# Seven products instead of eight for nine more projections of a four-layer network on one core, with hand-turned PSUM rings

## The chip, the cores and the metric

The kernel runs on one core of a Trainium2 chip. A core has five engines that run their own instruction queues side by side: TensorE (PE, matrix products into PSUM), VectorE (DVE), ScalarE (ACT), GpSimd (POOL) and SyncE (SP, which only starts transfers). All arithmetic is float32. The metric is the device time of one execution in microseconds (us); the lower the better.

## The reference

The input x has 4 images of 512 channels and 32 x 32 pixels, so an image is a matrix of 512 channels by 1024 tokens. Four layers follow one another, each of the form x = x + layer(groupnorm(x)):

```python
# layer 0: attention, heads mixed before the softmax, instance norm behind it
q, k, v = w_q @ xf, w_k @ xf, w_v @ xf            # 512x512 @ 512x1024 per image
attn = einsum('bhdq,bhdT->bhqT', q, k) * scale     # 8 heads of 64 channels
attn = softmax(einsum('gh,bhqT->bgqT', w_head, attn))
attn = instance_norm(attn) * gamma + beta
out = (attn @ v).reshape(b, t, c) @ w_proj.T + b_proj
# layer 1: a gate per channel from channel means (a small simulated circuit)
# layer 2: plain attention
q, k, v = Wq @ x + bq, Wk @ x + bk, Wv @ x + bv
out = Wp @ (softmax(q.T @ k * 64 ** -0.5) @ v) + bp
# layer 3: each token reads the 8 best of 2048 memory rows
att = q @ mempool.T; vals, idx = top_k(att, 8); out = softmax(vals) @ mempool[idx]
```

## The kernel before

An image lies in on-chip memory (SBUF) as 128 partitions x 4 channel blocks x 1024 tokens. A projection of an image by a 512 x 512 weight is 32 matmul statements of 512 columns (`project`, L184; `project_tokens`, L198, for v). For float32 each statement leaves two records in the profile.

**Layer 0** runs image after image in 32 steps of 32 queries plus 7 steps of tail (`step`). A step makes scores (`scores`), copies them out on ACT, sends them to another layout through 8 transfers (into the two relay buffers of tag `s2`), mixes the heads (`mix`), takes the exponential on ACT, turns it on DVE, and multiplies it into v five steps later (`apply`). Small products of gating, sums and norms go to one PSUM bank, `pt` (`small_ps`). In the tail steps 32 to 35 the next image's q is projected (`take_q`), one quarter a step; behind the tail comes its k (`take_k`, four projections, each copied out by one DVE instruction in the order that the scores want), and on DVE the statistics of the image after that (`statistics`: rows loaded into `xs` and `o1` by ACT's queue, one at a time). v follows in the first eight steps of the next image. After image 3's tail the projections are already those of layer 2's image 0 (`take_q2`, `take_k2`, `take_v2`), and then comes layer 0's output projection for image 3 (`put_out`, 64 statements of 256 columns), whose sums go straight into rows `xr`.

**Layer 2** runs over 16 units of 4 key blocks an image (`scores2`, `apply2`): scores on PE, exponential on ACT, sums over keys on POOL and DVE. Between the images the next one's projections are made: q with eight products (`take_q2`), k, v and the output projection with seven (`seven_k`, `seven_v`, `seven_out`).

**Seven products.** A matrix product of 2 x 2 blocks normally takes 8 block products; `seven` makes it of 7, from sums and differences of the blocks of both factors (Strassen's scheme). `input_sums` makes the sums of the image's blocks and `weight_sums` those of the weight, all on DVE; `seven` then runs products 1, 4, 3, 5, 2, 7, 6, each into one PSUM pair, and adds or subtracts it into the blocks of the result: the first into a block is written by `begin` (ACT or DVE, with the bias), the others by DVE (L993). Sums of weights are stored to memory for the later images.

**PSUM** has 8 banks. In layer 0 six of them are three named pairs that the code turns by step number (`pairs[at % 3]`), one is `pv` (the product with v) and one `pt`. In layers 2 and 3 a pool of three pairs and a pool of two banks take their place, and the pool hands them out in order.

The order on each engine is the order of the program for instructions wrapped in `pin`; the others may be moved by the scheduler. A wait is a semaphore wait at the head of an instruction, and everything behind it on that engine waits too. Transfers signal on eight lanes in turn; a transfer waits until the last user of its lane has landed.

Of the kernel before, what the change touches and what calls it, by code (L numbers as in the profile page):

```python
# [16 lines left out]
P = 128  # L17
# [24 lines left out]
def fast_net(ctx: ExitStack, tc: tile.TileContext, a: dict, out: bass.AP, flag: bass.AP):  # L42
# [19 lines left out]


    def chan(src, name):
        t = const.tile([P, KC], F32, tag=name, name=name)
        nc.scalar.dma_start(out=t, in_=src)
        return t

    gamma = const.tile([P, NH], F32, tag="gamma", name="gamma")
    nc.scalar.dma_start(out=gamma, in_=a["in_gamma"].partition_broadcast(P))  # L70
    beta = const.tile([P, NH], F32, tag="beta", name="beta")
    nc.scalar.dma_start(out=beta, in_=a["in_beta"].partition_broadcast(P))
    bproj = chan(a["b_proj"], "bproj")
    bq2 = chan(a["bq"], "bq2")
    bk2 = chan(a["bk"], "bk2")
    bp2 = chan(a["bp"], "bp2")
    fcb = chan(a["fc_b"], "fcb")

    fcw = const.tile([NQ, C], F32, tag="fcw", name="fcw")
    nc.scalar.dma_start(out=fcw, in_=a["fc_w"])  # L80
    qpar = const.tile([P, NL * NQ], F32, tag="qpar", name="qpar")
    nc.scalar.dma_start(out=qpar, in_=a["q_params"].partition_broadcast(P))
# [3 lines left out]
    ident = const.tile([P, P], F32, tag="ident", name="ident")  # L86
    make_identity(nc, ident)
    ones = const.tile([P, P], F32, tag="ones", name="ones")
    nc.gpsimd.memset(ones, 1.0)
# [13 lines left out]
    )  # L103
    NS = 32
# [71 lines left out]
    def place(at, name):  # L176

        return pairs[at % 3] if at is not None else ps_s.tile([P, 2, NB], F32, tag="sc", name=name)
# [107 lines left out]

    def run_out(gen):
        for _ in gen:
            pass
# [4 lines left out]
    def first():  # L294
# [3 lines left out]
        w = I["w_q"] = eight_k([P, KC, C], "w_q0_0", 0)  # L298
        for k in range(KC):
            nc.sync.dma_start(out=xn[:, k, :], in_=x_v[0, :, k, :])  # L300
            nc.sync.dma_start(out=w[:, k, :], in_=a["w_q"][:, k, :])
        I["w_k"] = load_w("w_k", "w_k0_0", 1)
# [5 lines left out]
        def stats(k):  # L308
            mv = small.tile([P, 2], F32, tag="mv0", name=f"mv0_{k}")
            st = small.tile([P, 2, 6], F32, tag="bnst", name=f"st_a0_{k}")  # L310
            for i in range(2):
                pin(nc.vector.bn_stats(st[:, i, :], xn[:, k, i * NB:(i + 1) * NB]))
            pin(nc.vector.bn_aggr(mv, st.rearrange("p i s -> p (i s)")))
            parts[k] = group_coeffs_parts(mv[:, 0:1], mv[:, 1:2], f"a0_{k}")

        def means(k):
            next(parts[k])
            next(parts[k])

        def deviations(k):  # L320
            next(parts[k])
            found[k] = next(parts[k])
# [15 lines left out]
        stats(0)  # L338
        means(0)
        stats(1)  # L340
        deviations(0)
        means(1)
        normalize(0)
        for k in range(KC):
            if k + 2 < KC:
                stats(k + 2)
# [634 lines left out]
    def load2(b):  # L981
        for key in ("Wq", "Wk", "Wv"):
            load_sums(b, key, b == 1 or key == "Wq")

    def load_sums(b, key, plain):
        w = img[b][key] = eight_k([P, KC, C], f"{key}2_{b}")
        nc.sync.dma_start(out=w, in_=a[key] if plain else w_sums[key])

    H = C // 2
    w_sums = {key: dram.tile([P, KC, C], F32, tag=f"ws_{key}", name=f"ws_{key}")  # L990
              for key in ("Wk", "Wv", "Wp")}
# [15 lines left out]
    def weight_sums(b, key):  # L1007
# [4 lines left out]
        add7(s1, a11, a22)  # L1012
        sub7(s7, a12, a22)
        add7(a12, a11, a12)
        sub7(s6, a21, a11)
        add7(a21, a21, a22)
        nc.sync.dma_start(out=w_sums[key], in_=w)

# [14 lines left out]
    def seven(b, key, src, multiply, view, block, begin, done=None):  # L1033
# [1399 lines left out]
```

## Time and profile before

| | us |
|---|---|
| runs (3) | 2554.56, 2555.19, 2558.83; median 2555.19 |
| the profiled execution | 2558.39 |
| its span, first to last instruction | 2556.6 |

The profile is of one execution; "busy" is the time in which an engine had an instruction under way, and the granted clock of TensorE is 0.998 of full. The table gives busy us in some stretches of the span:

| stretch, us from the start | what runs | PE | DVE | ACT | POOL |
|---|---|---|---|---|---|
| 265 to 345 (80) | layer 0, from image 0 to 1 | 78.41 | 28.35 | 14.63 | 20.40 |
| 345 to 550 (205) | layer 0, image 1 | 201.40 | 161.59 | 130.13 | 110.30 |
| 1215 to 1300 (85) | from layer 0 to layer 2 | 82.68 | 35.10 | 22.61 | 23.11 |
| 1300 to 1380 (80) | layer 2, image 0 | 80.00 | 55.88 | 43.35 | 55.78 |
| 1380 to 1490 (110) | layer 2, from image 0 to 1 | 108.04 | 67.61 | 16.67 | 20.66 |
| 1600 to 1710 (110) | layer 2, from image 1 to 2 | 110.00 | 61.48 | 18.01 | 13.75 |

A line such as "PE pv L532 <- ACT pv L592: 8.9, 15, 1.6" in the list of waits says that the matmuls of line 532 waited 8.9 us in total, 15 times and at most 1.6 us, for ACT's instruction of line 592.

### The profile page before, as it was taken

To read this page: it belongs to the slowest core of one execution; us is meant where nothing else is said; L and a number is where in the kernel's file an instruction comes from. 1 tells how busy PE (TensorE), PEld (TensorE's weight loads), DVE (VectorE), ACT (ScalarE), POOL (GpSimd) and SP (SyncE) were. 2 spreads that over 40 slices of the span, in tenths; PEclk is the share of its full clock that TensorE was granted. 3 is DMA by queue.
4 is the path that set the end of the run, shared out by engine and by line. 5 is a ranking of instruction groups with operands and counts; after the bars stand their busy time and mean duration, and the time that the engine had idled before them with its cause. 6 is when DMAs were issued, how large, how long until landed. Compare 5 with 4: busy or idle time off the path is not lost.

```text
span 2556.6 us, 47828 instructions
## 1 busy us (share of the span) xinstructions
PE 2503.3 (98%) x18534; PEld 1180.8 (46%) x18534; DVE 1685.8 (66%) x2785; ACT 985.8 (39%) x1177; POOL 1192.5 (47%) x1700
## 2 busy tenths in 40 slices
PE   8999999999999999999999999999999999999998
PEld 3344534554355534555633533453353344444445
DVE  4599448872688438881267567576657648788875
ACT  1467336651666336651153145125314612121211
POOL 3266415553465425553074147117405617566655
PEclk9999999999999999999999999999999999999999
DMA  2578438872698428982301130121014046767665
GB/s 83 145 207 237 125 120 226 244 211 74 172 243 235 131 82 211 244 248 101 124 16 55 70 112 18 54 83 59 21 54 148 18 130 190 219 186 217 187 184 170
DMA packets 187211, 361.39 MB, mean 141 GB/s; under 512 B 32729, under 2 KB 96217, under 8 KB 182882
## 3 DMA queue, kind: packets, MB, share of 16 engines
q1 hardware_dynamic: 105744, 178.71, 22.6%
q0 software_dynamic: 49152, 142.79, 20.6%
q10 hardware_dynamic: 32082, 36.76, 5.3%
q8 instruction: 149, 2.44, 0.4%
q14 instruction: 84, 0.69, 0.1%
HBM read 186.96 MB, written 36.96 MB: 88 GB/s over the span
## 4 chain that ended last, share of the span: by engine, by line
PE 74%; issue 10%; POOL 7%; DVE 3%; ACT 3%; DMA 2%; POOLq 0%; SPq 0%; ACTq 0%; DVEq 0%
PE pair L192 10%; PE sc_c L1183 9%; PE pv_c L1220 9%; PE pv L532 8%; POOL got L1360 7%; PE pair L467 6%; PE pair L493 5%; PE pt L425 5%; PE pt L721 4%; PE q L192 3%; PE Wk L1056 3%; PE Wv L1063 3%; ACT e L500 2%; PE Wp L1056 2%; PE at L1335 2%
## 5 line engine op out<-in xcount | busy, mean ns | idle before, releaser
L482 POOL DMA_DIRECT2D s<-ss x512 | 258.2, 511 | 399.5 <-PE pair L493 113.4
L506 DVE STREAM_TRANSPOSE eT<-e 128x1024 f32<-128x1024 f32 x256 | 316.5, 1236 | 193.6 <-ACT e L500 193.0
L1360 POOL DMA_INDIRECT got<-in_mem,ix x256 | 279.5, 1092 | 213.2 <-issue 122.1
L1177 ACT ACTIVATE eT<-sc_c 128x1024 f32<-128x1024 f32 x256 | 248.0, 1022 | 330.7 <-PE sc_c L1183 204.8
L521 DVE BATCH_NORM_STATS2 st<-e 128x6 f32<-128x256 f32 x1024 | 350.7, 404 | 0.0
L500 ACT ACTIVATE e<-pair 128x1024 f32<-128x1024 f32 x256 | 250.7, 1022 | 167.5 <-PE pair L493 137.2
L1201 POOL TENSOR_TENSOR e<-eT 128x1024 f32<-128x1024 f32 x96 | 232.3, 2421 | 168.6 <-DVE out L1125 69.5
L467 PE MATMUL pair<-k,q 64*32 64x512 f32 x4096 | 267.4, 598 | 12.7 <-ACT e L500 12.7
L473 ACT COPY ss<-pair 128x1024 f32<-128x1024 f32 x256 | 247.3, 1020 | 77.5 <-DMA s<-ss 37.9
L532 PE MATMUL pv<-eT,v 128*64 128x128 f32 x4096 | 250.7, 276 | 8.9 <-ACT pv L592 8.9
L532 PEld LDWEIGHTS pv<-eT,v 128*64 128x64 f32 x4096 | 221.1, 137 | 76.7 <-issue 54.5
L1183 PE MATMUL sc_c<-q,k 64*128 64x512 f32 x1024 | 240.9, 607 | 3.1 <-DVE xr L684 2.3
L1220 PE MATMUL pv_c<-eT,v 128*64 128x512 f32 x1024 | 233.0, 597 | 0.0
L1202 DVE TENSOR_TENSOR eT<-eT,e 128x1024 f32<-128x1024 f32 x96 | 136.3, 1420 | 146.3 <-POOL e L1201 146.1
L1197 POOL TENSOR_TENSOR eT<-eT 128x1024 f32<-128x1024 f32 x32 | 77.8, 2433 | 206.8 <-ACT eT L1177 202.8
L1407 DVE SCALAR_TENSOR_TENSOR acc<-got,et,acc 128x512 f32<-128x512 f32 x210 | 157.9, 752 | 7.5
L493 PE MATMUL pair<-s,wmix 32*32 32x512 f32 x4096 | 160.6, 600 | 2.3 <-issue 2.1
L1183 PEld LDWEIGHTS sc_c<-q,k 64*128 64x128 f32 x1024 | 93.6, 187 | 141.0 <-issue 71.9
L1340 ACT COPY att<-at 128x1024 f32<-128x1024 f32 (+1 forms) x65 | 64.9, 999 | 219.7 <-PE at L1335 212.9
L467 PEld LDWEIGHTS pair<-k,q 64*32 64x32 f32 x4096 | 57.0, 105 | 179.9 <-ACT e L500 86.2
L1220 PEld LDWEIGHTS pv_c<-eT,v 128*64 128x64 f32 x1024 | 68.0, 137 | 136.8 <-issue 136.8
L1335 PE MATMUL at<-memT,xn_d 128*128 128x512 f32 x256 | 120.7, 594 | 0.0
(335 smaller groups left out, 3431.3 us busy)
## 6 DMA issues: line engine op xcount, KB each, us to landing
s<-ss SPq DMA_DIRECT2D x512, 128.0 KB
s<-ss POOLq DMA_DIRECT2D x512, 128.0 KB
rb<-r POOLq DMA_DIRECT2D x64, 128.0 KB
o<-o SPq DMA_DIRECT2D x32, 256.0 KB
xr<-in_x ACTq DMA_DIRECT2D x32, 256.0 KB
x<-xr SPq DMA_DIRECT2D x32, 256.0 KB
xr_c<-x SPq DMA_DIRECT2D x32, 256.0 KB
rb_c<-r SPq DMA_DIRECT2D x64, 128.0 KB
```

Source lines behind the costliest of these rows:

```text
L192: pin(nc.tensor.matmul(ps[:, n, :], w[:, k, m * P:(m + 1) * P], rhs(k, n), start=(k == 0), stop=(k == KC - 1),))
L467: pin(nc.tensor.matmul(sc[m * NS:(m + 1) * NS, r, :], q[r * HD:(r + 1) * HD, m, s * NS:(s + 1) * NS], k_[r * HD:(r + 1) * HD, m, n * NB:(n ...
L482: pin(relays[side].dma_start(out=s2[2 * m + r::NH], in_=ss[m * NS:(m + 1) * NS, r, :]))
L493: pin(nc.tensor.matmul(mixed(s, r // 2)[t * NS:(t + 1) * NS, r % 2, :].rearrange("p (qq k) -> p qq k", qq=2), wmix[r * NS:(r + 1) * NS], s ...
L500: pin(nc.scalar.activation(e[:, half].rearrange("p r qq k -> p (r qq k)"), flat2(mixed(s, half)), AF.Exp))
L506: pin(nc.vector.transpose(eT[:, j % 2].rearrange("p b (qq i r) x -> p i r qq b x", qq=2, i=4)[:, i, 2 * half:2 * half + 2], e[:, half].rea ...
L521: pin(nc.vector.bn_stats(st[:, i, 2 * half + r, qq, :], e[:, half, r, qq, :]))
L532: pin(nc.tensor.matmul(pv[r * HD:(r + 1) * HD, gp, :], I["v"][:, t, g * HD:(g + 1) * HD], eT[:, j % 2, t, :, 4 * g:4 * g + 4], start=(t == ...
L1177: pin(nc.scalar.activation(e, scs[len(es)], AF.Exp))
L1183: pin(nc.tensor.matmul(sc[:, r, :], I["k"][r * HD:(r + 1) * HD, m, t * P:(t + 1) * P], I["q"][r * HD:(r + 1) * HD, m, n * NB:(n + 1) * NB] ...
L1220: pin(nc.tensor.matmul(pv[r * HD:(r + 1) * HD, :], I["v"][:, t, h * HD:(h + 1) * HD], e[:, r, :], start=(t == 0), stop=(t == TC - 1),))
L1360: pin(nc.gpsimd.indirect_dma_start(out=got[:, i, :], out_offset=None, in_=a["mem"], in_offset=bass.IndirectOffsetOnAxis(ap=ix[:, i:i + 1], ...
```

## The change

Four things change.

1. **Seven products** replace eight in nine more stages: k of images 1 to 3 in layer 0 (`seven_keys`; the factor sums of `sums_k` lie in the two relay buffers, which are free in the tail, and two of them are made anew in the same place during the stage, so that the image itself stays whole for v); k and v of layer 2's image 0 (`seven_by_channels`, `seven_v`); the output projection of layer 0's image 3 (`seven_collected`, with `output_sums`); and q of layer 2's images 1 to 3. q then carries no SCALE; the exponential applies it. The sums are spread over the steps before and between the products. Sums of Wq and three more sums for Wq and Wp are stored and loaded again.
2. **PSUM** keeps the pairs and banks of layer 0 to the end. `next_pair` turns a ring of three pairs, `next_bank` alternates `pv` and `pt`; with `late` the ring takes the other pair first. At the borders of layer 2 small products go to a single bank.
3. In the tail steps `take_out` (ACT's copy of `pv`) comes ahead of the next image's q; at a border of layer 2 the last unit's `apply2` comes ahead of q instead of behind it, and its sums over keys behind that.
4. **The start**: the first chunk of x is loaded in two halves, small constants are listed behind the first loads, the group statistics of image 0 run on DVE alone but for the power, and 17 small matmuls of ones are put ahead of and between the first products.

```diff
+    def next_pair(late=False):
+        if late:
+            ring[0:2] = ring[1::-1]
+        ring.append(ring.pop(0))
+        return pairs[ring[-1]]
...
+        for n in range(2):
+            nc.sync.dma_start(out=xn[:, 0, n * NB:(n + 1) * NB], in_=x_v[0, :, 0, n * NB:(n + 1) * NB])
         for k in range(KC):
-            nc.sync.dma_start(out=xn[:, k, :], in_=x_v[0, :, k, :])
+            if k > 0:
+                nc.sync.dma_start(out=xn[:, k, :], in_=x_v[0, :, k, :])
             nc.sync.dma_start(out=w[:, k, :], in_=a["w_q"][:, k, :])
+        for load in later:
+            load()
...
+            pin(nc.vector.tensor_sub(dm, mv[:, 0:1], ps[:, 0:1]))
+            pin(nc.vector.scalar_tensor_tensor(sq, dm, dm, mv[:, 1:2], ALU.mult, ALU.add))
...
+        def warm(times):
+            for _ in range(times):
+                pin(nc.tensor.matmul(pairs[2][:, 0, 0:P], ones, ones, start=True, stop=True))
...
+        warm(11)
+        for i in range(2):
+            stats(0, i)
         means(0)
-        stats(1)
+        stats(1, 0)
+        warm(2)
         deviations(0)
+        stats(1, 1)
+        warm(2)
+        normalize(0)
         means(1)
-        normalize(0)
+        warm(2)
...
         factors = {1: (s1, t1), 2: (s2, b11), 3: (a11, t3), 4: (a22, t4),
                    5: (s5, b22), 6: (s6, t6), 7: (s7, t7)}
+        factors |= own or {}
         for i, (at, uses) in enumerate(SEVEN):
-            ps = ps_s.tile([P, 2, NB], F32, tag="sc", name=f"{key}_{b}_{at}")
+            ps = next_pair()
...
+    def sums_k(b):
+        two = [apool.tile([P, 2, 2, NB], F32, tag="s2", bufs=2, name=f"sk_{b}_{i}") for i in range(2)]
+        t1, t3, t4 = places7["in"] = two[0][:, 0], two[0][:, 1], two[1][:, 0]
...
+        img[b]["own7"] = lambda: {6: (one, t4), 7: (other, t1)}
+        for ops in (
+                ((add7, t1, b11, b22), (add7, one, a11, a22)), ((sub7, t4, b21, b11),),
+                ((sub7, t3, b12, b22),), ((sub7, other, a12, a22), (add7, a12, a11, a12)), (),
+                ((sub7, one, a21, a11), (add7, a21, a21, a22), (add7, t1, b21, b22)),
+                ((add7, t4, b11, b12),)):
+            for fn, *places in ops:
+                fn(*places)
+            yield
+
+    def seven_keys(b):
...
+        def put(op, i, j, ps):
+            for m in range(2):
...
+                if op == "=":
+                    pin(nc.scalar.copy(to, of))
+                else:
+                    (add7 if op == "+" else sub7)(to, to, of)
+        ring[:] = [2, 0, 1]
...
+    def seven_collected(b):
...
+        def begin(i, j, ps):
+            for m in range(2 * i, 2 * i + 2):
+                pin(nc.scalar.activation(
+                    dst[:, m, j * NB:(j + 1) * NB], ps[:, m % 2, :],
+                    AF.Identity, bias=bproj[:, m:m + 1]))
+        def done(i, j):
+            for m in range(2 * i, 2 * i + 2):
+                part = dst[:, m, j * NB:(j + 1) * NB]
+                add7(part, part, rows.pop((m, j)))
+                pin(nc.vector.bn_stats(I["stb"][:, m, j, :], part))
...
-            pin(nc.scalar.activation(e, scs[len(es)], AF.Exp))
+            pin(nc.scalar.activation(e, scs[len(es)], AF.Exp, scale=SCALE))
...
-            sc = ps_s.tile([P, 2, NB], F32, tag="sc", name=f"sc_{nm}_{t}")
+            sc = next_pair(i >= 2 and u == UNITS2[b > 0])
...
             apply(b, s - LAG)
+        if s >= STEPS and tiled and part == 3:
+            take_out(b, j)
         if not tiled or s >= STEPS:
             piece(b, s)
...
-        if tiled and part == 3:
+        if tiled and part == 3 and s < STEPS:
             take_out(b, j)
...
+            if last and s == STEPS + 3:
+                border_places()
+                first7, rest7 = input_sums(nxt["xn"])
+                of_k = weight_sums(0, "Wk", False)
+            if last and s >= STEPS + 3:
+                take7((first7 + (lambda: next(of_k),))[s - STEPS - 3])
+                if s == STEPS + 3:
+                    next(of_k)
+            if not last and s >= STEPS + 3:
+                if s == STEPS + 3:
+                    key_sums = sums_k(b + 1)
+                next(key_sums)
...
-        for m in range(KC):
-            ks[m](m + 1)
+        for m, _ in enumerate(() if last else seven_keys(b + 1)):
             next(state["behind"], None)
+            next(key_sums, None)
...
-            for i in range(TC // 2):
-                take_v2(0, i, i + 2)
-            for m in range(KC):
-                put_out(b, m, m)
+            sums7 = output_sums(b)
+            for i, _ in enumerate(seven_v(0)):
+                if i < 2:
+                    run_some(of_p, (2, 2)[i])
+                else:
+                    for fn in next(sums7):
+                        fn()
+            seven_collected(b)
...
+    def next_bank():
+        turns[1] += 1
+        return (pv_bank, pt_bank)[turns[1] % 2]
     def small_ps(name):
-        return ps_s.tile([P, 2 * NB], F32, tag="sc", name=name)
+        return (pv_bank, pt_bank)[(turns[1] + 1) % 2] if at_border[0] else flat2(next_pair())
...
+            if s == 9 and b == 0:
+                weights = weight_sums(1, "Wq")
+            if s >= 10 and b == 0:
+                next(weights, None)
+            if s == len(UNITS2) - 2 and not last:
+                run_out(ahead)
+                first7, rest7 = input_sums(img[b + 1]["xn"])
+                first7[0]()
...
-        for m in range(KC):
-            take_q2(b + 1, m)
...
+        for i, _ in enumerate(seven_by_channels(b + 1, "q", bq2)):
+            if 1 <= i < 3:
+                rest7[i - 1]()
```

## The prediction

> **What bounds the kernel.** I read the busy row first, then TensorE's waits, then the chain of waits that ended last, and last the DVE groups and the stretches around the change.
>
> ```profile
> PE 2503.3 (98%) x18534; PEld 1180.8 (46%) x18534; DVE 1685.8 (66%) x2785; ACT 985.8 (39%) x1177; POOL 1192.5 (47%) x1700
> ```
>
> TensorE (PE) is busy 2503.3 of 2556.6 us, so it idles for 53.3 us in all. A busy row alone can flatter it, so what matters is what the other 53 us wait for:
>
> ```profile
> PE pair L467 <- ACT e L500: 12.7, 57, 1.5
> PE pv L532 <- ACT pv L592: 8.9, 15, 1.6
> PE pt L145 <- DVE mv L313: 7.3, 1, 7.3
> ...
> PE sc_c L1183 <- DVE xr L684: 2.3, 1, 2.3
> ...
> PE Wk L1056 <- ACT k L1073: 2.0, 1, 2.0
> ...
> PE pt L651 <- POOL ssqh L648: 0.9, 1, 0.9
> ```
>
> (Total us, times, longest.) No wait is large; what TensorE does less of, the kernel gets back nearly whole. The chain of waits, in order of time, shows the projections as unbroken PE work (start, length, what):
>
> ```profile
> 311.12 27.66 PE pair L192 x64
> ...
> 1209.97 27.57 PE pair L204 x64
> 1237.54 27.64 PE pair L745 x128
> ...
> 1382.40 27.66 PE q L192 x64
> ...
> 1641.72 20.80 PE Wk L1056 x48
> 1662.52 24.17 PE Wv L1063 x112
> ```
>
> A float32 matmul statement leaves two records. Eight-product stages (L192, L204, L745) take 27.6 us; the seven-product form of layer 2 is already here, and costs 20.80/24 = 0.867 us a statement of 512 columns (L1056) and 24.17/56 = 0.432 of 256 (L1063), against 27.66/32 = 0.864 at L192. Shorter groups cost no more per column.
>
> **The sum, part by part** (against the profiled execution: span 2556.6, 1.8 outside it).
>
> *1. Products.* Nine stages go from eight products to seven: k of images 1 to 3 in layer 0; k and v of layer 2's image 0; the output projection of layer 0's image 3; q of layer 2's images 1 to 3. Each loses 4 of 32 statements: 27.66 - 28 x 0.867 = 3.4 us, nine times **30.6**. The instruction lists of the two builds agree: 48 statements of 512 columns fewer, 24 of 256 more, or 48 x 0.864 - 24 x 0.432 = 31.1.
>
> *2. What the seven products ask of DVE and ACT.*
>
> ```profile
> L993 DVE TENSOR_TENSOR k<-k,Wk 128x1024 f32<-128x1024 f32 x24 | 28.7, 1218 | 15.7 <-PE Wk L1056 12.2 <-ACT k L1073 3.5
> L414 DVE COPY k<-pair 128x1024 f32<-128x1024 f32 x16 | 19.5, 1223 | 80.8 <-PE pair L192 80.8
> ```
>
> Before, layer 0's k cost DVE four copies of 1.22 us and ACT nothing. After: 8 sums out of PSUM (8 x 1.22 = 9.8), 1.22 + 0.68 + 0.68 + 1.22 of factor sums still due inside the stage (3.8), statistics of the next image as before (8 x 0.68 + 4 x 0.21 = 6.3): 20 us beside 24.3 of PE. The other factor sums (5.7 us) stand in steps 35 to 38, where DVE idles 13.5 us before its reciprocal (L559). A PSUM pair comes round after three products, 10.4 us, so DVE may lag 6.9. Walking the queue from 309.4 (the new start), the loads of xs, whose issue on ACT now has copies of k queued behind it, put DVE some 6 us late at the fourth product; its pair is free at 329.2, wanted at 330.2. The last sum ends near 336.3; the value matmuls (3.5 us) and first scores cover it until 338. Cost taken 0; if that cover fails, 1 to 2 us for each of images 1 and 2 (image 3 has no statistics).
>
> At the border to layer 2 the v stage asks DVE for 12 x 1.22 + four weight sums at 0.68 + twenty sums of 256 columns at about 0.4 (near the 0.44 of L684), 25 us beside 24.2, and the output stage 9.8 + 8 x (0.68 + 0.69) + 0.8 = 21.6. By the same walk DVE ends the output stage 5 to 6 us after PE. Layer 2's first scores take the other two pairs meanwhile (that is what the swap of the ring does), and reach the late one 7 us later: 0 again. These scores also no longer wait for DVE's last add (sc_c <- xr): **+2.3**.
>
> In layer 2 the sums for Wq are five adds of 0.68, and t1 one of 1.22, inside the attention units of image 0 (only t1 for images 1 and 2). [...]
>
> ```profile
> L1260 DVE SCALAR_TENSOR_TENSOR seen<-ri_c,seen 128x32 f32<-128x32 f32 x64 | 61.1, 955 | 1.1
> L561 DVE SCALAR_TENSOR_TENSOR seen<-ri,seen 128x32 f32<-128x32 f32 x64 | 17.3, 270 | 2.2
> L1202 DVE TENSOR_TENSOR eT<-eT,e 128x1024 f32<-128x1024 f32 x96 | 136.3, 1420 | 146.3 <-POOL e L1201 146.1
> ```
>
> The same 32-column operation takes 955 ns among POOL's adds and 270 elsewhere; the 1024-column add 1420 against 1218 at the border. [...] By the 1024-column row each pays 0.2. I take the row: L1202 itself waits 146/96 = 1.5 us for POOL each time, idle into which an add fits. 0, with up to 5 us in the range.
>
> *3. Waits that go.* In step 34, ACT copies q (L292) before pv (L592), so step 35's apply waits 1.59, 1.54 and 1.5 us in images 0 to 2 (timeline). Taking pv out ahead of the q piece puts that copy under 7 us of q matmuls: **+4.6**; the copies of q behind it come 0.6 later and release nothing soon. The other 4 us of that group lie in the main loop and stay. At the first border of layer 2 k's second product waits 2.0 for ACT's bias copies, since two small products (L1251, L145) each took a pair of the ring between them and it came round early; they go to a single bank now: **+2.0**. The instance norm runs between products, so L651's 0.9 goes: **+0.9**.
>
> *4. A wait that comes.* In step 35 of image 3, t1 and a weight sum (1.22 + 0.68) stand on DVE ahead of the reciprocal that frees the small PSUM bank. It starts near 1175.4 instead of 1173.5; the gating matmul (1174.2 before) waits for it, and behind it on PE stand 3.7 us of apply and all of k: **-1.5**.
>
> *5. The start.* Nothing multiplies before 11.31 us. SP's row says why loads are late:
>
> ```profile
> SPq L301 <- DMA bproj<-in_b_proj: 6.1, 1, 6.1
> ```
>
> Loads share eight completion lanes, and a load waits for the lane's last user. In the new build x's second chunk waits for gamma (landed about 5.7, when ACT's bp goes), where before it went at 1.73: landing near 8.5 to 9 for 8.1. The first chunk comes in halves and its POOL steps (0.19 each) become DVE steps: about 0.8 earlier. The third chunk (13.78 before, which set the matmuls of the second chunk at 17.04) waits for w_q's first and lands about 12. And 17 small matmuls are put ahead to warm PE. The first four product records took 3.78 us for 1.83 later. [...] Either way the next product waits for the third chunk, so I take **+1.0** between -0.8 and 2.5. gamma and its like are not wanted before circuit(); their place costs nothing else.
>
> *6. No cost.* SCALE moves from q's addition into the exponential's own scale, the same instructions. Extra weight-sum transfers (three of 256 KB each way) go by SP, whose row holds nothing late in layer 2, and DMA is 13 to 24% busy there.
>
> Sum: 30.6 + 2.3 + 4.6 + 2.0 + 0.9 - 1.5 + 1.0 = 39.9. Span 2516.7; from the runs' median, 2555.2 - 39.9 = **2515.3**.
>
> **Rivals.**
> *A: DVE becomes the bound at the borders.* For: 25 us asked in 24.2, and loads of xs between DVE's sums. Against: a lag is forgiven up to 6.9. Losing 3 us at each of three borders gives 2524.
> *B: the products alone count*: the waits of part 3 come back elsewhere (pv's on the exponential, L467), the start gains nothing: 2555.2 - 30.6 + 1.5 = 2526.
> *C, slower: the hand ring makes each attention unit wait.* If the fixed order put a score behind an exponential of its own unit (1.02, L1177) in 64 units, 65 us would be lost: 2580. It decides from 39.9/64 = 0.62 us a unit. Against: the ring turns over three pairs as the pool did, and the new list has 232 score groups with waits where the old had 254.
> *D: seven products cost more than the rows say* (factor sums not ready): bounded by L1056's 0.867 and its one wait; inside A.
>
> **Chances.** Main case 0.72 (2509 to 2520), A 0.13, B 0.11, C 0.03, no gain 0.01. The range, 2508 to 2526, takes in A, the start's ends and most of B. A measurement of this kernel tells 0.2% (5 us) from no change: faster 0.96, same 0.01, slower 0.03.
>
> **What would show it.** 24.3 us stages in place of 27.6 at nine places; the 1.5 us waits of pv gone (about 4 left of 8.9); sc_c <- xr and Wk <- k gone; a new wait of the gating matmul on DVE's reciprocal near 1174; the second chunk's first matmul near 15.5 to 16.5. Wrong if PE shows waits of over 1 us on DVE sums (L993's successor) at the borders, or on the exponential in layer 2's units.

## The result: half of the predicted gain

Six runs of the changed kernel have a median of 2535.4 us (2534.53 to 2539.42), six of the kernel before, on the same chip, 2555.98 (2553.91 to 2559.15): a ratio of 0.9921 (0.9909 to 0.9932). About 20 us are gained where 39.9 were predicted. The profiled execution took 2539.05 us with a span of 2537.3, which is 19.3 less than before.

The busy row after, to be read against that of before:

```profile
PE 2482.0 (98%) x18520; PEld 1177.2 (46%) x18520; DVE 1803.6 (71%) x2940; ACT 1019.2 (40%) x1237; POOL 1217.8 (48%) x1688
```

TensorE idles 55.3 us (2537.3 - 2482.0), 2 more than before, though the warm-up products fill 7.6 us that were idle at the start: elsewhere the waits grew by some 10 us. It is busy 21.3 us less where 31 us of products were taken out; the warm-up is 7.6 us of that difference, and the lower mean granted clock, 0.996 for 0.998, adds to it. The list of TensorE's waits (total us, times, longest) says where to look:

```profile
PE pair L510 <- ACT e L543: 12.8, 56, 1.5
PE pair L536 <- DMA s<-ss: 5.4, 4, 2.4
PE pt L934 <- POOL amp L926: 5.4, 3, 2.5
PE pt L152 <- DVE eT L1452: 5.0, 2, 2.6
PE pv L575 <- ACT pv L635: 4.0, 11, 1.0
PE pt L944 <- POOL pr L939: 1.9, 2, 1.0
...
PE pt L929 <- DVE ri L602: 1.4, 1, 1.4
...
PE pt L1395 <- DVE eT L1452: 1.1, 1, 1.1
...
PE pair L1358 <- DVE sum L1041: 0.9, 1, 0.9
...
PE pair L1112 <- DVE sums L1041: 0.7, 1, 0.7
```

The waits that the prediction named as going are gone or where it left them: pv (L575) is down from 8.9 to 4.0. New or longer are L934, L152 and L944. All three are products of a few columns into a small bank, of the gating or of a group norm, queued between the big products. In the list of the kernel before, only the first of them stands, as L891, and with one short wait:

```profile
PE pt L891 <- POOL amp L883: 0.6, 1, 0.6
```

The chain of waits shows the stages themselves, three of them here:

```profile
310.16 24.23 PE pair L1112 x56
...
606.53 7.06 PE pair L1112 x16
614.57 10.50 PE pair L1112 x24
...
1208.47 24.17 PE pair L1238 x112
```

The seven products of k for image 1, and of v at the border to layer 2, run unbroken in 24.2 us, as predicted. Those for image 2 are in pieces, and their first two products are not among the pieces at all: there the chain runs through other engines. DVE's rows of layer 2, by line and form:

```profile
L1377 DVE TENSOR_TENSOR eT<-eT,e 128x1024 f32<-128x1024 f32 x96 | 142.5, 1485 | 129.4 <-POOL e L1376 129.2
...
L1435 DVE SCALAR_TENSOR_TENSOR seen<-ri_c,seen 128x32 f32<-128x32 f32 x64 | 56.8, 887 | 1.1
```

The units' own addition on DVE went from 1420 to 1485 ns a time, and from 146.3 to 129.4 us of idle time before it: the sums added there take a little from it (experiment 10). The 32-column operation (L1435) did not slow: 887 ns for 955 before.

Laid side by side by stage (us saved; each measured between the same instructions in both traces):

| stage | predicted | saved |
|---|---|---|
| start, and layer 0's image 0 up to the next q | 1.0 | -0.7 |
| border into image 1 (first q product to first v product): 70.86 to 65.77 | 5.0 | 5.1 |
| border into image 2: 74.31 to 73.22 | 4.9 | 1.1 |
| border into image 3: 74.30 to 73.21 | 4.9 | 1.1 |
| layer 0's loops of images 1, 2, 3 | 0 | -4.3 |
| from layer 0 to layer 2's first scores: 131.8 to 123.3 | 11.9 | 8.5 |
| layer 2, from there to image 0's output projection: 203.7 to 200.2 | 5.4 | 3.4 |
| from one output projection to the next: 219.1 to 218.2, 219.1 to 217.9 | 6.8 | 2.1 |
| the rest | 0 | 3.0 |

The first border is the clue. No gating runs at it (that of an image runs behind the tail of the next), and it gained all that was predicted. The next two have the same products and gained 1.1.

### What stands at the border into image 2

The timeline of the changed kernel there (start, length, engine, line, operation, idle before it and the releaser):

```profile
590.25 0.39 PE L929 MATMUL pt<-amp,turn 128*128 128x4 f32 x2
...
590.75 3.04 DVE L1041 TENSOR_TENSOR sk<-xn_all 128x1024 f32<-128x1024 f32 x2
...
591.68 2.48 POOL L922 TENSOR_SCALAR ampt<-amp,sincos 128x4 f32<-128x4 f32 x2
...
595.49 0.19 POOL L926 TENSOR_TENSOR amp<-ampt 128x2 f32<-128x2 f32 x1
595.74 0.30 PEld L934 LDWEIGHTS pt<-amp,turn 128*128 128x128 f32 x2 [1.70 <-POOL amp L926]
595.74 0.38 PE L934 MATMUL pt<-amp,turn 128*128 128x2 f32 x2 [1.45 <-POOL amp L926]
...
596.20 5.38 PE L1112 MATMUL pair<-sk,sk 128*128 128x512 f32 x8
...
602.05 3.60 POOL L648 TENSOR_TENSOR o<-pv,rb 64x256 f32<-64x256 f32 x4
...
605.73 0.20 POOL L939 TENSOR_TENSOR pr<-amp 128x4 f32<-128x4 f32 x1
...
605.98 0.35 PE L944 MATMUL pt<-pr,signs 128*9 128x1 f32 x8 [0.97 <-POOL pr L939]
```

and the same steps of the gating in the kernel before, in its timeline (L891 is L934, L896 is L939, L901 is L944):

```profile
595.64 0.59 POOL L879 TENSOR_SCALAR ampt<-amp,sincos 128x4 f32<-128x4 f32 x2
...
597.55 0.19 POOL L883 TENSOR_TENSOR amp<-ampt 128x2 f32<-128x2 f32 x1
...
598.18 0.38 PE L891 MATMUL pt<-amp,turn 128*128 128x2 f32 x2
...
607.48 0.20 POOL L896 TENSOR_TENSOR pr<-amp 128x4 f32<-128x4 f32 x1
...
612.56 0.35 PE L901 MATMUL pt<-pr,signs 128*9 128x1 f32 x8
```

A chain goes TensorE, DVE, POOL, TensorE: L929, a copy, L922 to L926, L934. Two POOL instructions of four columns took 0.59 us before; beside two of DVE's 1.5 us sums of inputs they took 2.48. L934 is late by 1.45, and with it all of k, which is queued behind it. Then the first product takes 5.38 us where 3.70 is normal (experiment 1). The chain goes on over POOL to L944, which waits 0.97; before, its operand was ready about 5 us before TensorE came to it. The stretches of that place say why the first product is slow (the first number behind POOL's is the granted clock):

```profile
594.00:598.00 4.00, 2.55 (x13) 1.30 (x10) 1.56 (x3) 0.59 (x1) 3.50 (x11) 0.88 0.13 43
598.00:604.00 6.00, 6.00 (x13) 2.52 (x12) 0.00 (x0) 2.05 (x4) 5.22 (x17) 0.80 0.18 61
```

In steps of 0.5 us the clock is 0.50 from 597.0 to 600.4 and 1.00 on both sides. The span of the changed kernel has five such drops, at 9.9, 259.1, 597.0, 887.2 and 1180.7, each 3.41 us long; that of the kernel before has two, at 1267.7 and 2544.3 (in both, one more runs past the last instruction and is left out). A drop under products costs half its length, 1.7 us: 5.38 for 3.70.

### The profile page after: what moved, and what is told of

The parts are those of the page before. It is cut to its first block, busy times and chain, and to the rows that moved or that the text cites. A ratio compares the mean times of both kernels' runs of the same rounds, so it can differ in the third digit from the quotient of the medians.

```text
span 2537.3 us, 48070 instructions
## 1 busy us (share of the span) xinstructions
PE 2482.0 (98%) x18520; PEld 1177.2 (46%) x18520; DVE 1803.6 (71%) x2940; ACT 1019.2 (40%) x1237; POOL 1217.8 (48%) x1688
## 4 chain that ended last, share of the span: by engine, by line
PE 65%; issue 10%; POOL 10%; DVE 7%; DMA 5%; ACT 2%; SPq 0%; POOLq 0%; ACTq 0%; DVEq 0%
PE pair L1112 11%; PE pair L1358 7%; PE pv L575 7%; PE pair L199 7%; POOL got L1535 7%; PE pair L510 6%; PE pair L536 5%; PE pt L468 5%; PE pair L1238 4%; PE pt L1395 4%; PE pt L764 3%; PE pv L1395 3%; DMA s<-ss 2%; ACT e L543 2%; DVE eT L1377 1%
## 5 line engine op out<-in xcount | busy, mean ns | idle before, releaser
L1352 ACT ACTIVATE eT<-pair 128x1024 f32<-128x1024 f32 x256 | 248.2, 1022 | 319.9 <-PE pair L1358 158.0
L1376 POOL TENSOR_TENSOR e<-eT 128x1024 f32<-128x1024 f32 x96 | 240.4, 2507 | 166.8 <-ACT eT L1352 122.3
L510 PE MATMUL pair<-k,q 64*32 64x512 f32 x4096 | 268.1, 600 | 12.8 <-ACT e L543 12.8
L575 PE MATMUL pv<-eT,v 128*64 128x128 f32 x4096 | 250.7, 276 | 4.0 <-ACT pv L635 4.0
L575 PEld LDWEIGHTS pv<-eT,v 128*64 128x64 f32 x4096 | 221.1, 137 | 71.7 <-issue 55.2
L1358 PE MATMUL pair<-q,k 64*128 64x512 f32 x1024 | 240.0, 605 | 2.0 <-DVE sum L1041 0.9
L1377 DVE TENSOR_TENSOR eT<-eT,e 128x1024 f32<-128x1024 f32 x96 | 142.5, 1485 | 129.4 <-POOL e L1376 129.2
L1372 POOL TENSOR_TENSOR eT<-eT 128x1024 f32<-128x1024 f32 x32 | 83.4, 2606 | 201.3 <-ACT eT L1352 197.4
L536 PE MATMUL pair<-s,wmix 32*32 32x512 f32 x4096 | 160.9, 602 | 6.9 <-DMA s<-ss 5.4
L1358 PEld LDWEIGHTS pair<-q,k 64*128 64x128 f32 x1024 | 92.2, 186 | 140.4 <-issue 66.4
L1515 ACT COPY att<-pair 128x1024 f32<-128x1024 f32 (+1 forms) x65 | 64.9, 999 | 221.2 <-PE pair L1510 212.4
L1041 DVE TENSOR_TENSOR k<-k,pair 128x512 f32<-128x512 f32 (+1 forms) x80 | 67.9, 893 | 78.3 <-PE pair L1112 62.1
L1530 DVE MAX8 top<-att 128x8 f32<-128x2048 f32 x31 | 71.1, 2293 | 73.0 <-issue 40.8
L1510 PE MATMUL pair<-memT,xn_d 128*128 128x512 f32 x256 | 120.7, 594 | 0.0
```

Of the source, the lines that this page charges most:

```text
L510: pin(nc.tensor.matmul(sc[m * NS:(m + 1) * NS, r, :], q[r * HD:(r + 1) * HD, m, s * NS:(s + 1) * NS], k_[r * HD:(r + 1) * HD, m, n * NB:(n ...
L536: pin(nc.tensor.matmul(mixed(s, r // 2)[t * NS:(t + 1) * NS, r % 2, :].rearrange("p (qq k) -> p qq k", qq=2), wmix[r * NS:(r + 1) * NS], s ...
L575: pin(nc.tensor.matmul(pv[r * HD:(r + 1) * HD, gp, :], I["v"][:, t, g * HD:(g + 1) * HD], eT[:, j % 2, t, :, 4 * g:4 * g + 4], start=(t == ...
L1352: pin(nc.scalar.activation(e, scs[len(es)], AF.Exp, scale=SCALE))
L1358: pin(nc.tensor.matmul(sc[:, r, :], I["k"][r * HD:(r + 1) * HD, m, t * P:(t + 1) * P], I["q"][r * HD:(r + 1) * HD, m, n * NB:(n + 1) * NB] ...
```

## The experiments

Times are medians, beside the kernel before on the same chip. "The borders" are the stages of the table above into images 2 and 3 (73.2 and 73.2 us in the changed kernel).

**1. The gating's second product behind the first k product** (gate_held).

```diff
-            step(b, s, lambda b, s: next(state["behind"], None),
+            step(b, s, lambda b, s: s < STEPS + LAG - 1 and next(state["behind"], None),
```

> The gating of the image before is held back by one step in the last step of each image's tail, so its second small product (L934) is queued behind the first of the seven k products instead of ahead of it. Theory A (the missing gain at the layer 0 borders is one late small product and what it sets off): the wait of L934 (1.45, 1.47 and 2.49 us in images 1, 2 and 3) is covered by the 3.5 us product, the granted clock does not drop to 0.50 at those three places, the first k product takes 3.5 instead of 5.4 us; worth 3 x 1.7 for the clock and 5.4 for the waits, so 8 to 10 us, total near 2526. Rival B (the products themselves are slow at the border, because VectorE and the transfers are busy there): the wait moves behind the first product, which still takes about 5.4 us; at most 3 us gained, total near 2533. Rival C (the gating is late anyway): the same 5 us of waits appear at L934 or L944 later; no gain.

Measured: 2542.2 (before 2555.65; ratio 0.9949, 0.9929 to 0.9968). The borders take 72.2 and 73.8, so nothing is gained. Theory A missed and rival C is what happened. The timeline:

```profile
590.43 3.70 PE L1112 MATMUL pair<-sk,sk 128*128 128x512 f32 x8
...
596.62 4.10 POOL L648 TENSOR_TENSOR o<-pv,rb 64x256 f32<-64x256 f32 x4
...
600.83 1.93 POOL L922 TENSOR_SCALAR ampt<-amp,sincos 128x4 f32<-128x4 f32 x2
...
604.60 0.35 PE L944 MATMUL pt<-pr,signs 128*9 128x1 f32 x8 [3.16 <-POOL pr L939]
```

L934 no longer waits and the first product is back at 3.7. But POOL now has the scaling of the output (L648) ahead of the gating's L922 as well as of its L939, and the third group of small products waits 3.16 us, and 4.18 in image 3.

**2. The two sums of inputs one product later** (sums_moved).

```diff
-                ((add7, t1, b11, b22), (add7, one, a11, a22)), ((sub7, t4, b21, b11),),
-                ((sub7, t3, b12, b22),), ((sub7, other, a12, a22), (add7, a12, a11, a12)), (),
+                ((add7, t1, b11, b22), (add7, one, a11, a22)), (), (),
+                ((sub7, other, a12, a22), (add7, a12, a11, a12)), ((sub7, t4, b21, b11), (sub7, t3, b12, b22)),
```

> The two differences of inputs (1.5 us of VectorE each) that run beside the gating's GpSimd chain in the tail are made one product later, behind the first k product; everything else as in the changed kernel. Theory A1 (these VectorE instructions hold up the GpSimd chain: its two L922 took 2.48 us beside them, 0.56 where VectorE was idle): L922 takes 0.6 to 1.1 us, the wait of L934 falls from 1.45 to under 0.4 in images 1 and 2, and with it the clock drop; 2 x (1.3 + 1.7) = 6 us less, total near 2529; the lost time may come back in part at the second product, which now waits for a difference. Rival A2 (the GpSimd chain is late because GpSimd is full of its own work, the output scaling): L934 still waits 1.4 us and the total stays within 2 us of 2535.

Measured: 2541.35 (ratio 0.9937, 0.9918 to 0.9957); borders 75.6 and 76.0. The cause of the first wait is what A1 says: in the timeline L922 is back at 0.59 and L934 does not wait. The total missed, since the next wait is longer:

```profile
590.64 0.59 POOL L922 TENSOR_SCALAR ampt<-amp,sincos 128x4 f32<-128x4 f32 x2
...
595.61 1.12 POOL L623 TENSOR_TENSOR sqs<-sqs,st 128x64 f32<-128x64 f32 x1
596.81 1.11 POOL L624 TENSOR_TENSOR sqs<-sqs 128x32 f32<-128x32 f32 x1
...
604.60 0.20 POOL L939 TENSOR_TENSOR pr<-amp 128x4 f32<-128x4 f32 x1
```

Now DVE's sums hold up POOL instructions that stand ahead of the gating's in its queue (L623 and L624 took 0.41 and 0.25 in the changed kernel), L648 stands ahead of L939 as in the changed kernel (3.58 us for 3.60), and L944 waits 4.11.

**3. TensorE kept at work through the wait** (filled).

```diff
         def second(ps):
+            for _ in range(0 if by_scalar else 6):
+                pin(nc.tensor.matmul(ps[:, P:2 * P], ones, ones, start=True, stop=True))
```

> Six products of ones by ones into unused columns of the same bank are queued ahead of L934 in images 1 to 3, to keep TensorE at work in the wait; nothing else changes and the wait in time is the same. Theory A (the drop of the granted clock follows from the idle time): no drop at 0.50 near 597 and 887 us, the first k product takes 3.5 us instead of 5.4; 2 to 3 times 1.7 us gained, 3.4 to 5.2 us, total near 2531. Rival B (the first product is slow from contention): it stays at 5.4 us and the six products add up to 1 us each time; total 2535 to 2538.

Measured: 2541.0 (ratio 0.9948, 0.9929 to 0.9967); borders 74.8 and 74.7. The first product took 3.68 at full clock, as theory A said, but L944 then waited 2.77 instead of 0.97, and the clock fell there. The 1.7 us were only moved to the next wait for POOL. At the border to layer 2 the same wait grew to 4.94, and that stage took 128.7.

So experiments 1 to 3 agree: at this border the chain through POOL has a length of its own, and TensorE is queued to meet it too early, wherever one shortens TensorE's side. Counted from the start of L934 into image 2, in us:

| kernel | end of L939 (operand ready) | TensorE stands at L944 | L944 waits |
|---|---|---|---|
| before | 9.5 | 14.4 | 0 |
| changed | 10.2 | 9.3 | 0.97 |
| gate_held | 10.6 | 7.5 | 3.16 |
| sums_moved | 11.6 | 7.6 | 4.11 |
| filled | 10.3 | 7.6 | 2.77 |

The changed kernel's 9.3 is 7.6 and the 1.7 of the drop: the slow first product hides part of the wait.

**4. The chain of small products in layer 2 one product later** (norm_held).

```diff
                 run_out(weight_sums(1, "Wk"))
-            next(behind, None)
+            if i > 0: next(behind, None)
```

> At the layer 2 borders the chain of small products starts behind the second q product instead of the first. Theory D (the first small product, L152, waits for its bank, which VectorE's late output multiplication L1452 still reads: 2.65 and 2.33 us at the borders 1 to 2 and 2 to 3): both waits go under 0.3, the time falls by 4 to 5 us, total near 2531. Rival E (TensorE waits there for VectorE anyway, since VectorE is behind with sums of factors): the q products wait in its place for a difference of inputs or a buffer; gain under 1.5 us.

Measured: 2529.05 (ratio 0.9893, 0.9874 to 0.9911). Theory D: L152's waits are gone from the list, and from one output projection to the next it takes 215.3 both times, 3.8 less than before. What it had waited for, in the changed kernel's timeline:

```profile
1597.22 1.08 SPq L1440 DMA_DIRECT2D rb_c<-r  x2
...
1600.89 0.69 DVE L1452 TENSOR_TENSOR eT<-pt,rb_c 128x512 f32<-128x512 f32 x1 [1.36 <-DMA rb_c<-r]
...
1601.64 0.39 PE L152 MATMUL pt<-mv_d,gavg 128*128 128x4 f32 x2 [2.65 <-DVE eT L1452]
```

The bank given to the small products is the one whose last product with v DVE still has to multiply (L1452), and that waits for a transfer.

**5. The changed kernel again** (after_again).

> The changed kernel as it is, on the same chip as the other runs of this call. Theory A: the late small products come back at the same places with the same waits (L934 1.4 us twice and 2.5 us, L152 2.6 and 2.3), since their instruction order makes them; the waits of the mixing product for its transfers inside the image loops (2.4, 1.0, 1.5 and 2.0 us in the first profile) change by a microsecond or more or are gone, if they are chance. Rival F (the change itself delays those transfers): these waits stand at the same four places again, 6 to 7 us in all. Total 2535 to 2542.

Measured: 2536.79 (before 2554.28; ratio 0.993, 0.9911 to 0.9949). L934 waits 1.45, 1.46 and 2.48, L152 2.60 and 2.20. Into image 3 the clock did not fall this time; there L944 waited 2.64 instead of 0.95, and the border took 73.2 as with the drop. At these two borders the drop is thus no loss of its own: what it costs, L944 waits less (norm_held, into image 2: no drop, L944 2.65, border 73.2).

Of the waits for the mixing product's transfers, one over 0.9 us is left (1.05), and the loops of images 1 to 3 take 0.8 us more than before instead of 4.3. So most of those 4.3 us are scatter: in total these waits are 1.1 to 5.4 us in the traces of the changed kernel and its variants, and 5.4 also in experiment 6, which puts no sums into the relay buffers. Whether the change adds a little there stays open, since the one trace of the kernel before puts none of its waits down to these transfers.

**6. The old eight products for k of images 1 to 3** (old_keys).

```diff
...
-        for m, _ in enumerate(() if last else seven_keys(b + 1)):
+        for m in range(0 if last else KC):
+            ks[m](m + 1)
             next(state["behind"], None)
-            next(key_sums, None)
```

The sums of factors in the tails of images 0 to 2 go with them (a condition above these lines becomes `False`).

> k of images 1 to 3 by eight products of quarters as in the kernel before, and no sums of factors in the tails of images 0 to 2; the rest as in the changed kernel. The seven products alone are worth 3.4 us at each of three borders, so without theory A this kernel is 10 us slower than the changed one (2545). Theory A (at images 1 and 2 the late gating and the clock drop eat what the seven products save): at the border before image 1, where no gating runs, 3.4 us are lost; at the other two L934 no longer waits, no clock drop follows, and they lose 0 to 0.5 us; total 3 to 5 us above the changed kernel, 2539 to 2541.

Measured: 2541.73 (ratio 0.995, 0.9933 to 0.9966), 4.9 above the changed kernel. The border into image 1 takes 69.19, which is 3.4 more; the other two take 72.76, which is 0.5 *less* than with seven products. L934 and L944 do not wait at these two: the operand is ready 9.5 us after L934, and TensorE comes to L944 after 14.4. This is the plainest result: where the gating runs, the seven products are worth nothing as they were placed, and where it does not run, all that was predicted.

**7. The gating's steps spaced** (spaced): experiment 1, and

```diff
-            next(state["behind"], None)
+            if m not in (2, 3): next(state["behind"], None)
```

in both stages of k, and a step behind v products 3 to 7 in the last image.

> The gating's steps are spaced: none in the last step of the tail, then behind k products 1, 2, 5, 6 and 7 (in the last image also behind v products 3 to 7), so that each small product has about as much time behind the step before as it had between two of the four old k chunks. Theory G (the chain on GpSimd takes some 10 us at the border whatever TensorE does, and TensorE comes to its small products too early since the steps follow every 3.5 us instead of every 7): no wait of L934 or L944 over 0.3 us, no clock drop at the three borders; 1.45 + 1.47 + 2.49 + 1.9 of waits and 3 x 1.7 of clock, 12 us less than the changed kernel on the same chip, near 2524. Rival H (the time moves on once more): a new wait of 2 us or more at L944 or L959, gain under 5 us.

Measured: 2530.78 (ratio 0.9912, 0.9896 to 0.9929), 6.0 under the changed kernel. TensorE's timeline at the border into image 2:

```profile
591.06 3.70 PE L1112 MATMUL pair<-sk,sk 128*128 128x512 f32 x8
594.60 0.28 PE L934 MATMUL pt<-amp,turn 128*128 128x2 f32 x2
...
601.91 7.03 PE L1112 MATMUL pair<-xn_all,w_k_n 128*128 128x512 f32 x16
608.87 0.35 PE L944 MATMUL pt<-pr,signs 128*9 128x1 f32 x8
```

L934 and L944 do not wait, and the clock does not drop: the operand is ready 10.6 us after L934, TensorE comes after 14.3. Two short waits are left behind them, 0.51 for L955 and 1.14 for the gate ahead of v. The borders take 70.64 and 69.39, that to layer 2 119.0 (124.9 in after_again): 12.2 less, as theory G said. Half of it came back, as H warned, but elsewhere: at layer 2's first border the chain of small products now begins with another norm, meets the busy bank of experiment 4, and waits 3.63 with a drop of the clock behind it (206.4 instead of 200.2 us to the output projection).

**8. Spaced, experiment 4, and four more warm-up products** (spaced_all; `warm(2)` ahead of `normalize(0)` becomes `warm(6)`).

> The spaced gating, the layer 2 chain of small products starting one q product later, and four more warm-up products at the start, where TensorE idled 1.6 us and the clock fell to 0.50 at 9.9 us. If the three causes are separate, the gains add: 12 + 5 + 1.7 us under the changed kernel on the same chip, near 2517, which is what the prediction named (2515). Rival: the start is bound by the arrival of the second chunk and gains nothing from the clock, near 2519; or one of the waits is replaced by another, over 2522.

Measured: **2523.1** (before 2554.28; ratio 0.9878, 0.9861 to 0.9894), 13.7 under the changed kernel on the same chip. The sum of 18.7 was not reached. The return of experiment 7 is gone (200.2). In the profiled execution (span 2520.0) the border into image 3, the way to layer 2 and the two stages between output projections gain 4.9, 12.8 and 7.6 us against the kernel before, where 4.9, 11.9 and 6.8 were predicted; into image 2 it is 3.7, with the wait of 1.14 for the gate and a drop behind it. The start gained nothing: the drop at 9.9 moved to 17, where two waits of 1.0 and 1.1 us for the third chunk stand.

**9. Experiment 8 with the start of the changed kernel, and in the last image a later gating as well** (spaced_best). The added edit:

```diff
-            step(b, s, lambda b, s: next(state["behind"], None),
+            step(b, s, lambda b, s: s < STEPS + LAG - 1 - last and next(state["behind"], None),
```

> The spaced gating and the later chain of small products at the layer 2 borders together, with the start as in the changed kernel, and in the last image of layer 0 the gating held for the last two steps of the tail instead of one, since its first small product there (L929) waited 1.43 us for a VectorE instruction queued behind a sum of factors. If theories A, D and G hold and are separate: the border of image 3 falls by another 1.4 us to about 117.6, the other borders of layer 0 stay at 70.6 and 69.4, those of layer 2 (from one first product of Wp to the next) at 215.3; total 2520 to 2524. Rival: the later start of the gating in image 3 only moves its steps into layer 2, where they cost the same again; 2524 to 2528.

Measured: 2521.93 (before 2555.68; ratio 0.9863, 0.9846 to 0.9879). Not told apart from experiment 8. The added step missed: L929 still waits 1.43, a wait of 1.64 came at the instance norm (L694 for DVE), and the border to layer 2 takes 120.7 instead of 119.0.

**10. Layer 2's sums for Wq not on DVE** (wq_copied).

```diff
-            fn(out, x, y)
+            fn(out, x, y) if key != "Wq" else nc.sync.dma_start(out=out, in_=x)
```

> In the layer 2 units of image 0 the five sums of quarters of Wq (VectorE) are replaced by plain transfers of one of the two operands, so q of images 1 to 3 in layer 2 is not what it should be; everything else as in the changed kernel. [...]

Measured, one run: the units of image 0 take 118.4 instead of 119.8 and L1395's wait (1.05) is gone: beside POOL's additions of e these sums cost the units 1.4 us. The stage of q behind them gains another 1.0, since its second product no longer waits 0.70 for a sum of DVE (L1041). So the sums for Wq cost 2.4 us there.

**11 and 12. The clock alone** (z_held, z_held_filled): L944 three products later in images 1 and 2, without and with the six filling products of experiment 3.

```diff
-            next(state["behind"], None)
+            if m not in (1, 2, 3): next(state["behind"], None)
```

> As the changed kernel, but the gating's third group of small products (L944) follows the fifth k product instead of the second in images 1 and 2. L934 is where it was and waits 1.45 us again. With theory A the clock falls after it and the first k product takes 5.4 us; the borders into images 2 and 3 (first q product to first v product) take 73.2 less the 1 us that L944 waited, 72.2 us, if L944 itself is the only other loss.

> The same, with six products of ones queued ahead of L934, so that TensorE works through the wait. L934 comes at the same time. Theory A (the drop follows from the idle time and costs 1.7 us by itself): the first k product takes 3.7 us, no drop at 0.50 at either border, and with nothing left to wait for the borders are 1.7 us shorter than without the filling, 70.5 us. Rival (the drop comes from something else at this place, or the time is waited for later in any case): both borders within 0.3 us of those without the filling.

Measured, one run each: borders 72.27 and 72.63 without, 70.92 and 70.93 with. Into image 3 it went as theory A says. TensorE's timeline without the filling,

```profile
882.70 0.38 PE L934 MATMUL pt<-amp,turn 128*128 128x2 f32 x2 [1.47 <-POOL amp L926]
...
883.16 5.38 PE L1112 MATMUL pair<-sk,sk 128*128 128x512 f32 x8
```

and with it,

```profile
877.18 1.60 PE L935 MATMUL pt<-ones 128*128 128x128 f32 x12
878.72 0.38 PE L936 MATMUL pt<-amp,turn 128*128 128x2 f32 x2
...
879.18 3.68 PE L1114 MATMUL pair<-sk,sk 128*128 128x512 f32 x8
```

The small product comes at the same point, and the idle time before it costs 1.7 us more than itself. Into image 2 the expectation missed: the same wait of 1.47 brought no drop at all (first product 3.68), and the 1.35 us between the two runs there are mostly later waits: 0.59 for L955, which the other run has not, and 1.14 for the gate ahead of v, which is 0.48 there.

## Why the prediction was half right

*Part 1, products, 30.6:* right. Unbroken stages take 24.2 us, and experiment 6 gives 3.4 for one stage.

*Part 2, "The other factor sums (5.7 us) stand in steps 35 to 38, where DVE idles", cost 0:* **this is the step that failed first.** I asked whether DVE had time, not what its sums do to the POOL instructions beside them. And I read that time, like the walk of DVE's queue, at the border into image 1, where no gating runs; into image 2 the idle time is shorter and the gating stands in it:

```profile
305.76 0.36 DVE L559 RECIPROCAL ri<-pt 128x32 f32<-128x32 f32 x1 [13.54 <-PE pt L556]
...
592.44 0.36 DVE L559 RECIPROCAL ri<-pt 128x32 f32<-128x32 f32 x1 [10.48 <-PE pt L556]
```

DVE's adds beside POOL's I had weighed for layer 2's units alone, and by the 1024-column row (1420 ns for 1218) and DVE's idle time there I took them as 0. There they cost 2.4 us (experiment 10). It was in the tail of layer 0 that such an overlap decided, where POOL's instructions are short and on a chain to TensorE: 0.59 became 2.48, and 0.59 again when the sums were moved (experiment 2). The walk of DVE's queue through the k stage itself held; no product there waited for a sum.

*Part 4, "A wait that comes", -1.5 in image 3:* that one came (1.43), but the list was short by five others: L934 three times (5.4 us) and L944 twice (1.9). They are late for two reasons. L934 stands in the tail, where no product became shorter; DVE's sums delay it, into images 2 and 3 through L922 (experiment 2), and in the last image, as far as the trace shows, through the late L929 and through L648, whose two instructions took 3.41 us there beside the sums and 1.78 just before. L944 is a matter of distance. With seven products the gating makes a step every 3.5 us instead of every 7: TensorE came to L944 14.4 us after L934 before, and comes after 7.6 at full clock, while POOL still needs 10.2. Halving the distance used up that cover, and I did not count the queue of POOL between the steps. In the profiled execution this is 7.3 us of waits and some 5 of clock; where the clock does not fall, L944 waits 1.7 longer instead (experiment 5). Experiment 7 takes 12.2 back.

*Part 3, waits that go:* +4.6 for pv right. The +2.0 of "they go to a single bank now" is right for the border where I read it and forgot the others: the bank is busy there, 5.0 us at the next two borders (experiment 4). The +2.3 became 1.4, since the first scores now wait 0.93 for DVE's last sum.

*Part 5, the start, +1.0:* no run shows this term, a value that I took between two ends; the start saved 0.2, up to image 0's first v product (the table's -0.7 has image 0's loop in it). The warm-up did not bring the first products to full clock: TensorE idles 1.60 us from 8.18, the clock is 0.50 from 9.93 to 13.34, and the first four product records take 2.99 us, for 3.78 before and 1.96 for the next four. And the third chunk did not land near 12: its statistics on DVE begin at 13.72, for 13.78 before, so the second chunk's first product comes at 16.81 and not at 15.5 to 16.5.

Rival A named DVE at the borders, but as lateness with the big sums, which did not occur. Rival B, with 2526, was the nearest in kind: waits that come back elsewhere. It looked for them on the exponential, and had neither the small products nor the clock. The 3.0 us saved in the rest fall in layer 3 (508.7 us before, 505.4 after); 1.5 of them are a drop of the clock that the kernel before had there (its last 32 records of products took 5.33 us, 3.81 in the changed kernel), and the cause of the remainder stays open.

## What to carry to other kernels

When the big work between two steps of a slow side chain gets shorter, the chain's cover goes with it: count the side chain's own length, engine by engine and queue by queue, before counting the saving. A product of one column holds up everything queued behind it (L944, up to 4.94 us in experiment 3), so place it by the time its operand is ready, and place it with a bank that nobody still reads (L152, up to 2.65 us in the changed kernel). When one wait is removed and the time stays, look for the next instruction of the same chain (experiments 1 to 3) before giving up the theory: spacing all of it gave 12 us at the borders, where none of these three single moves gave any.

## What was not expected of the hardware

In these traces the granted clock falls by a fixed grid. Read in stretches of 0.05 us, the drops of the changed kernel begin at 9.93, 259.10, 597.02, 887.15 and 1180.70, and each lasts 3.413 (some in other traces last two such steps, 6.83, as in gate_held from 1187.0). First and last are 1170.77 us apart; as 343 steps that is 3.4133 us a step, and the distances are then 73.0, 99.0, 85.0 and 86.0 steps. The two drops of the kernel before, 1276.58 us apart, are 374.0 steps. In other executions the grid lies elsewhere (from the start of the span, 2.61 past a multiple in gate_held, 3.10 in the changed kernel). In the step before each of the five drops of the changed kernel TensorE idles 1.62, 2.02, 1.45, 1.47 and 2.49 us. In the fourteen traces of this case, from 40 us on, 31 idle times put more than 2.0 us into one step, and 30 of them were followed by a step at half clock (the other put in 2.00); in the changed kernel they are 2.02 before L536 and 2.49 before L934, in the kernel before 2.32 before L1183 and 2.17, in two pieces, before L1393. The 1.45 and 1.47 before L934 in the changed kernel were followed by one too. But waits of 1.5 us in the main loop were not (1.49 before L467 in the kernel before), nor were four that put 1.88 to 1.92 us into one step (1.89 before L1056 in the kernel before), nor, in z_held into image 2, the same 1.47 before L934. What decides between these cases, and whether small products count, stays open. In this kernel a wait of 1.5 us or more may cost 1.7 us beyond itself (5.38 for 3.68 in experiment 11), depending on where it falls and on whether a later wait takes it up. That is likely a part of the scatter between runs of one kernel: of gate_held's, the shortest took 2535.29 us at a mean granted clock of 0.998, the longest 2546.69 at 0.994.
